# Eight images through a spectral network and a dilation on one core: one more pair of the mixing inside layer 3, and ten head steps behind it in a new order

## The chip, the cores and the metric

The kernel runs on one core of a Trainium2 chip, all in float32. The metric is the device time of one execution in microseconds (us). Five engines work side by side, each through its own list of instructions: TensorE (PE: matrix multiplications; PEld: its weight loads), VectorE (DVE), ScalarE (ACT), GpSimd (POOL) and SyncE (SP). In this kernel SyncE and GpSimd only issue DMAs, but for the setup.

## The reference, cut to what matters

The input has eight images of 8 channels and 256 x 256 pixels. Each goes through a group norm, a network of four spectral layers with a two-stage head, a residual addition, and then another group norm and a 3 x 3 dilation with a second residual addition.

```python
h = _gconv1x1(concat(group_norm(x), grid), fc0_w, fc0_b)      # 40 channels in 4 groups
for i in range(4):
    h1 = irfft2(mix(low modes of rfft2(h), sp_w1[i], sp_w2[i]))   # 12 + 12 rows, 12 columns of modes
    h2 = _gconv1x1(h, w_w[i], w_b[i])
    h = h1 + h2
    if i < 3:
        h = _gswish(h, betas[i])
x = x + _gconv1x1(_gswish(_gconv1x1(h, fc1_w, fc1_b), betas[3]), fc2_w, fc2_b)
x = x + max over 3 x 3 neighbours of group_norm(x), border -2
```

## The kernel before

**Images and layers.** An image's hidden state `h` lies whole in SBUF, in 11 chunks. In each layer `burst(c)` makes a chunk: matrix multiplications with the state (L587 in layer 0, L590 later) and the inverse column transform (L593), then the activation on ScalarE (L598, or L600 in layer 3) back into `h`. In layers 0 to 2 transposes and forward transforms follow (L541, L558, L572). Between two layers stands the spectrum: `spectrum_h` (in front of layer 0, `spectrum_x`), then `mix`, which works out the product of modes and weights, then `rows_even` or `rows_odd`, which make the row transforms (p_g, L487 or L509) and copy them to `zt` (L215 to L217).

**The mixing.** `mix` has twelve operations on VectorE, n = 0 to 11, six pairs of a product (L411) and a sum (L414) of about 1 us each; then six small additions and subtractions that make `fs` (L432, L433); then the multiplications p_f (L455, L464) and copies into `fz` (L465 to L471).

**The head.** Layer 3 stores each chunk of its result to DRAM (L602). The head of that image reads it again as hidden states (L789: 44 of them in all, each for three first steps) and runs while the layers of the next image run. It has 128 *first* steps (`f`) and 64 *second* steps (`c` or `C`). A first step multiplies a state by the first weights into four banks of PSUM (L813) and applies the activation on ScalarE in two pieces, one bank (L814) and three banks (L815). A second step multiplies two activations by the second weights into one bank (L830). An addition on VectorE then takes this bank up into `y` (L837 where a row block begins, L839 else). With `c` the addition is put on VectorE's list at once; with `C` it waits in `sums_due` and is put there at the next first step, or at the next `c`. After each eighth addition statistics (L845) and a write to DRAM (L847, from GpSimd) follow.

**PSUM.** Its eight banks are two single ones (tag `one`) and two triples (tag `tri`), each used in turn. A first step takes one of each, a second step a single, p_f and the first row transform one of each. A user waits until the one two before it has been read.

**Who runs when.** `layers` is a generator for an image. Its yields are strings such as "ffc", and for each letter the main loop calls `step`, which runs a first or a second step of the oldest head that still has some; "t" runs a piece of the dilation of an image whose head is done. The lists of TensorE, VectorE, ScalarE and SyncE are in the order in which this program issues instructions; nothing reorders them later.

**The next image inside layer 3.** `start(b + 1, nxt)` is a second generator: `spectrum_x` and then `mix` with l = 0 of the next image, cut to pieces by its own yields, whose values don't matter here. `rows_odd` of layer 3 runs two of its pieces, and each chunk of layer 3 runs two more (two `next(side, None)` per chunk): 24 in all. What is left then runs in `rest`, behind layer 3: a piece, the head steps of `REST` for that place, some reads of the next image's pixels into the free chunks of `h` (`read_x`, L532, four DMAs a chunk, from SyncE), and so on. Layer 3 itself reads chunks 0 to 6 of the next image when a head runs beside it; for image 0, where none does, all 11 chunks are read in `rest`.

In the kernel before, 20 pieces are `spectrum_x` (the last of them is empty: two yields follow each other at its end, L353 and L354), four pieces hold the pairs n = 0,1 to 6,7, then four pieces hold one operation each (n = 8, 9, 10, 11), one the six additions, and the last one p_f and what follows. So `rest` begins with n = 8. The head steps in it, for images 1 to 6, are `f`, `fc`, `ffC`, `ff`, `fc`. The first `f` and the first `c` are the last of the old head; all others are of the new one.

Of the kernel before, what the change touches and what calls it, by code (L numbers as in the profile page):

```python
# [34 lines left out]
NCH = 11  # L35
# [4 lines left out]
DR = 2  # L40
STEPS = 128
BEHIND = mybir.DependencyInfo(mybir.DependencyClass.Sync, mybir.DependencyReason.DATA)
REST = ("ff", "f", "f", "fC", "fc"), ("f", "fc", "ffC", "ff", "fc")


@with_exitstack
def fno_dilate_kernel(ctx: ExitStack, tc: tile.TileContext, a: dict, out: bass.AP):
# [11 lines left out]
    def ps_a(name):  # L59
        return ps.tile([128, 512], F32, tag="one", bufs=2, name=name)  # L60
# [8 lines left out]
    def part(i):  # L69
        return slice(32 * i, 32 * i + 32)  # L70


    n_img = a["x"].shape[0]
    turned = const.tile([128, 3, 2048], F32, tag="turned", name="turned")

    def load_x(b):
        for i in range(2):
            nc.sync.dma_start(turned[:, i], a["xw"][b, :, i])
# [169 lines left out]
    def rsqrt(v, r, d):  # L248

        nc.vector.tensor_scalar(r.bitcast(I32), v.bitcast(I32), -0.5, float(0x5F3759DF), ALU.mult, ALU.add)  # L250
        nc.vector.tensor_scalar(v, v, -0.5, None, ALU.mult)
        for _ in range(4):
            nc.vector.tensor_tensor(d, r, r, ALU.mult)
            nc.vector.tensor_tensor(d, d, v, ALU.mult)
            nc.vector.scalar_tensor_tensor(r, d, 1.5, r, ALU.add, ALU.mult)


    def group_means(p, v):

        mm(p[:, 0:G], avg, v, start=True, stop=True)  # L260
        for g in range(G):
            mm(p[part(g), G : G + 1], avg[:, 0:32], v[:, g : g + 1], start=True, stop=True)


    def spectrum_x(b, out_):

        x = turned[:, 0:2].rearrange("p i (g f) -> p i g f", g=G)
        st = sb.tile([128, G, 2, 6], F32, tag="bn", bufs=1, name=f"bn_x{b}")
        for i in range(2):
            for g in range(G):  # L270
                nc.vector.bn_stats(st[:, g, i, :], x[:, i, g])
            yield
        mv = sb.tile([128, G, 2], F32, tag="mvx", name=f"mv_x{b}")
        for g in range(G):
            nc.vector.bn_aggr(mv[:, g], st[:, g].rearrange("p n s -> p (n s)"))
        yield
        yield
        yield
        p = ps_a(f"p_st_x{b}")
        group_means(p, mv[:, :, 0])  # L280
        mr = sb.tile([128, 2, G + 1], F32, tag="mrx", name=f"mr_x{b}")
        d = sb.tile([128, 2, G + 1], F32, tag="dx", bufs=1, name=f"d_x{b}")
        nc.vector.tensor_copy(mr[:, 0], p[:, : G + 1])
        dm = d[:, 0, :G]
        nc.vector.tensor_tensor(dm, mv[:, :, 0], mr[:, 0, :G], ALU.subtract)
        nc.vector.tensor_tensor(dm, dm, dm, ALU.mult)
        nc.vector.tensor_tensor(dm, dm, mv[:, :, 1], ALU.add)
        yield
        yield
        q = ps_a(f"p_sv_x{b}")  # L290
        group_means(q, dm)
        nc.vector.tensor_scalar(d[:, 1], q[:, : G + 1], EPS, None, ALU.add)
        rsqrt(d[:, 1], mr[:, 1], d[:, 0])
        out_["mr"] = mr[:, :, G]
        for g in range(G):
            nc.vector.tensor_scalar(
                x[:, :, g], x[:, :, g], mr[:, 0, g : g + 1], mr[:, 1, g : g + 1], ALU.subtract, ALU.mult)
            if g != 1:
                yield
        yield  # L300

        a1, a2 = turned[:, 2, 0:512], turned[:, 2, 512:1024]
        a3 = turned[:, 2, 1024:1216].rearrange("p (g m) -> p g m", g=G)
        nc.vector.memset(a3, 0.0)
        p = ps_a(f"p_a1_{b}")
        for i in range(2):
            for g in range(G):
                mm(p[part(g)], er[:, i, :], x[:, i, g], start=i == 0, stop=i == 1)
        nc.vector.tensor_copy(a1, p)
        yield  # L310
        yield
        t = ps_a(f"p_a2_{b}")
        for i in range(4):
            nc.tensor.transpose(t[:, 128 * i : 128 * (i + 1)], a1[:, 128 * i : 128 * (i + 1)], ident)
        nc.vector.tensor_copy(a2, t)
        yield
        yield
        p = ps_a(f"p_a3_{b}")
        for j in range(2):
            for i in range(2):  # L320
                mm(p[:, 24 * j : 24 * j + 24], a2[:, 256 * j + 128 * i : 256 * j + 128 * i + 128], fw[:, i, 0:24],
                   start=i == 0, stop=i == 1)
        for g in range(G):
            nc.vector.tensor_copy(a3[part(g), g, :], p[part(g), 0:48])
        yield
        yield
        cols = a3.rearrange("p g (j k) -> p g j k", j=2)
        p = ps_a(f"p_xs_{b}")
        for k in range(2):
            for term in range(2):  # L330
                for q in range(4):
                    k0 = 12 * term + 3 * q
                    mm(p[part(q), 24 * k : 24 * k + 24], unf[:, spectrum_table(k, term), :],
                       cols[:, :, :, k0 : k0 + 3], start=term == 0, stop=term == 1)
        xe4 = xe.rearrange("p (s k) g j -> p s g j k", s=2)
        for k in range(2):
            nc.vector.tensor_copy(
                xe4[:, k, :, 0:2, :],
                p[:, 24 * k : 24 * k + 24].rearrange("p (g j k) -> p g j k", g=G, j=2),
            )  # L340
        yield
        bt = sb.tile([128, 2, 3, G, WID], F32, tag="B", bufs=1, name=f"B_{b}_0")
        prod = turned[:, 0, :1200].rearrange("p (i g o j) -> p i g o j", i=6, g=G, o=WID)
        for i in range(6):
            nc.vector.tensor_tensor(
                prod[:, i], wext, xe[:, i].unsqueeze(2).to_broadcast([128, G, WID, 5]), ALU.mult
            )
        nc.vector.tensor_reduce(
            bt.rearrange("p s k g o -> p (s k g o)"),
            prod.rearrange("p i g o j -> p (i g o) j"), AX.X, ALU.add,  # L350
        )
        out_["bt"] = bt
        yield  # L353
        yield  # L354

    def spectrum_table(k, term):

        return 0 if k == term else (1 if k == 0 else 2)
# [44 lines left out]
    def mix(b, l, out_):  # L403
# [3 lines left out]
        for n in range(12):  # L407
            k, k2 = n // 4, n // 2 % 2
            pr = turned[:, 2, 1024 * k2 : 1024 * k2 + 800].rearrange("p (g m i) -> p g m i", g=G, i=WID)
            if n % 2 == 0:  # L410
                nc.vector.tensor_tensor(  # L411
                    pr, sw[k], bt[:, k2, k].unsqueeze(2).to_broadcast([128, G, 2 * WID, WID]), ALU.mult)
            else:
                nc.vector.tensor_reduce(  # L414
                    s[k2][:, k].rearrange("p s o g -> p (s o) g"),
                    pr.rearrange("p g m i -> p m g i"), AX.X, ALU.add,
                )
            if l == 0:
                if n % 2 or n > 7:
                    yield  # L420
            elif n not in (0, 2, 6, 10):
                yield {1: "fc", 4: "fC", 7: "fC", 9: "fC"}.get(n, "f")
            if n == 2 and l == 3 and b + 1 < n_img:
                load_x(b + 1)
# [104 lines left out]
    def read_x(b, c):  # L529
        if b < n_img:  # L530
            for g in range(G):
                nc.sync.dma_start(h[32 * g : 32 * g + 6, c].rearrange("p f w -> p (f w)"), a["xp"][b, c, g])  # L532
# [140 lines left out]
    def start(b, out_):  # L673
        if b < n_img:
            if b == 0:
                out_["sw"] = [load_sw(0, k) for k in range(3)]
            yield from spectrum_x(b, out_)
            yield from mix(b, 0, out_)

    def rest(b, then):  # L680
        c = 0 if b == 0 else NCH - 4
        for n, _ in enumerate(then):
            yield REST[b > 0][n]
            for _ in range(2 if b == 0 else 1):
                if c < NCH:
                    read_x(b + 1, c)
                    c += 1
        for i in range(c, NCH):
            read_x(b + 1, i)

    def layers(b, stored, d, then, ahead):

        for l in range(4):
            if l > 0:
                yield from spectrum_h(b, l, d)
                yield from mix(b, l, d)
            yield from rows_odd(b, l, then) if l % 2 else rows_even(b, l)  # L700
            yield from layer(b, l, d, stored, then, ahead)
        yield "stored"
        yield from rest(b, then)
# [420 lines left out]
```

## Time and profile before

| what | us |
|---|---|
| median of 3 runs (lowest, highest) | 3690.49 (3689.13, 3691.84) |
| the profiled execution: its time, its span | 3688.73, 3687.0 |
| PE busy | 3486.2 |
| ACT busy | 2865.0 |
| DVE busy | 2386.8 |
| one product of the mixing (L411), one sum (L414), mean | 0.983, 0.984 |
| one addition of the head (L839), mean | 0.684 |
| activation of a first step: L814, L815, mean | 0.602, 1.458 |

Times in the profile count from the start of the span. A line of the timeline gives the start, the length from the first to the last of the merged instructions, the engine and the line of the kernel, the operation, what it writes and reads, how many were merged, and in brackets how long the engine was idle before and what ended this. SPq is SyncE's queue; the length of its issues holds what it waits between them. An engine that waits for several things has the wait put down to the one that came last.

### The profile page before, as it was taken

The numbers are of one execution on the slowest core, as the hardware profiler recorded it, in microseconds if no ns is written. First come the engines' busy times: TensorE is split into PE (matmuls) and PEld (weight loads), VectorE is DVE, ScalarE is ACT, GpSimd is POOL, SyncE is SP. The second block draws the span as 40 slices with busy tenths as digits, with TensorE's granted clock in tenths as the row PEclk, the third lists the DMA queues.
The fourth block names the chain that finished last, engine by engine and source line by source line (L and its number), as shares of the span: only waits on it lengthen the run. The fifth ranks groups of instructions, "written<-read, shape, count | busy, mean of one in ns | idle before, by whom it ended". The sixth has DMA issues, their size and how long they took to land.

```text
span 3687.0 us, 112658 instructions
## 1 busy us (share of the span) xinstructions
PE 3486.2 (95%) x50872; PEld 1270.1 (34%) x50872; DVE 2386.8 (65%) x3711; ACT 2865.0 (78%) x3021; POOL 117.1 (3%) x202
## 2 busy tenths in 40 slices
PE   5768999999999999999999999999999999999997
PEld 2323333333333333333333333333333333333222
DVE  6776666557775677757776577765777567772443
ACT  2436888888788788787888888888888888889986
POOL 1000000000000000000000000000000000000000
PEclk7879999999999999999999999999999999999998
DMA  3005111532226212271224512253222521225221
GB/s 92 16 17 212 49 50 46 165 106 72 72 84 195 68 58 72 87 226 53 65 57 138 170 55 75 64 168 114 67 73 89 189 75 58 71 65 193 84 82 48
DMA packets 114080, 344.71 MB, mean 93 GB/s; under 512 B 15984, under 2 KB 18480, under 8 KB 98176
## 3 DMA queue, kind: packets, MB, share of 16 engines
q1 hardware_dynamic: 95392, 276.32, 24.5%
q0 software_dynamic: 18208, 61.18, 5.1%
q8 instruction: 400, 6.55, 0.7%
q14 instruction: 80, 0.66, 0.1%
HBM read 213.44 MB, written 123.74 MB: 91 GB/s over the span
## 4 chain that ended last, share of the span: by engine, by line
PE 73%; DVE 16%; issue 5%; ACT 4%; DMA 2%; POOL 0%; ACTq 0%; DVEq 0%; POOLq 0%
PE p_fc L830 20%; PE p_fc L813 19%; PE p_z L593 9%; PE p_d L558 7%; PE p_z L590 7%; PE p_z L587 3%; DVE y L839 3%; PE p_u L572 3%; DVE turned L541 3%; DVE S L414 3%; DVE turned L411 2%; DMA yin<-y_rows 2%; DVE turned L372 1%; PE p_b L381 1%; PE p_g L509 1%
## 5 line engine op out<-in xcount | busy, mean ns | idle before, releaser
L815 ACT ACTIVATE act<-p_fc 128x1536 f32<-128x1536 f32 x1024 | 1493.2, 1458 | 0.0
L813 PE MATMUL p_fc<-hs,c_w 32*128 32x512 f32 x8192 | 1133.4, 625 | 41.2 <-DVE y L839 20.8
L830 PE MATMUL p_fc<-act,c_w 128*32 128x512 f32 x8192 | 1007.0, 600 | 0.2 <-ACT act L815 0.2
L814 ACT ACTIVATE act<-p_fc 128x512 f32<-128x512 f32 x1024 | 616.6, 602 | 228.2 <-PE p_fc L813 216.8
L541 DVE STREAM_TRANSPOSE turned<-h 128x1024 f32<-128x1024 f32 x528 | 632.6, 1226 | 189.7 <-ACT h L598 189.0
L598 ACT ACTIVATE h<-p_z 128x512 f32<-128x512 f32 (+1 forms) x528 | 511.9, 1021 | 213.9 <-PE p_z L593 213.9
L839 DVE TENSOR_TENSOR y<-p_fc,y 128x512 f32<-128x512 f32 x392 | 267.9, 684 | 539.1 <-PE p_fc L830 539.1
L813 PEld LDWEIGHTS p_fc<-hs,c_w 32*128 32x128 f32 x8192 | 358.3, 183 | 613.4 <-ACT act L814 253.3
L830 PEld LDWEIGHTS p_fc<-act,c_w 128*32 128x32 f32 x8192 | 221.4, 109 | 703.9 <-issue 330.8
L593 PE MATMUL p_z<-c_binv,zt 32*128 32x256 f32 x5632 | 410.3, 405 | 0.0
L590 PE MATMUL p_z<-h,c_wt 32*32 32x512 f32 x8448 | 357.8, 601 | 7.9 <-ACT act L814 4.2
L593 PEld LDWEIGHTS p_z<-c_binv,zt 32*128 32x128 f32 x5632 | 258.9, 186 | 308.0 <-issue 295.1
L558 PE MATMUL p_d<-turned,c_fw 32*32 32x480 f32 (+1 forms) x9216 | 307.6, 539 | 0.6 <-DVE turned L541 0.2
L562 ACT ACTIVATE turned<-p_d 128x1440 f32<-128x1440 f32 x144 | 183.0, 1271 | 89.5 <-PE p_d L558 86.3
L600 ACT ACTIVATE h<-p_z,c_bias 128x512 f32<-128x512 f32 (+1 forms) x176 | 186.4, 1110 | 72.0 <-PE p_z L593 71.8
L215 ACT ACTIVATE zt<-p_g 128x198 f32<-128x198 f32 (+2 forms) x118 | 53.4, 575 | 182.7 <-PE p_g L487 99.9
L414 DVE TENSOR_REDUCE S<-turned 128x80 f32<-128x800 f32 x192 | 189.0, 984 | 5.9
L411 DVE TENSOR_TENSOR turned<-t,B 128x800 f32<-128x800 f32 x192 | 188.7, 983 | 0.9
L558 PEld LDWEIGHTS p_d<-turned,c_fw 32*32 32x32 f32 x9216 | 127.1, 103 | 165.6 <-issue 64.7
L372 DVE STREAM_TRANSPOSE turned<-zt 128x960 f32<-128x960 f32 x96 | 176.8, 1867 | 2.5
L590 PEld LDWEIGHTS p_z<-h,c_wt 32*32 32x32 f32 x8448 | 92.9, 103 | 175.3 <-DVE y L839 48.8
L572 PE MATMUL p_u<-turned,c_stack 128*32 128x480 f32 (+1 forms) x1152 | 136.7, 543 | 11.5 <-DVE turned L561 6.2
(192 smaller groups left out, 1763.1 us busy)
## 6 DMA issues: line engine op xcount, KB each, us to landing
stored<-h SPq DMA_DIRECT2D x88, 1024.0 KB
hs<-stored SPq DMA_DIRECT2D x352, 256.0 KB
t<-in_spw SPq DMA_DIRECT2D x96, 400.0 KB
yin<-y_rows POOLq DMA_DIRECT2D x56, 512.0 KB, 5.2
h<-in_xp SPq DMA_DIRECT2D x352, 48.0 KB
turned<-in_xw SPq DMA_DIRECT2D x16, 1024.0 KB
y<-in_x SPq DMA_DIRECT2D x56, 256.0 KB
y_rows<-y POOLq DMA_DIRECT2D x56, 256.0 KB, 4.0
```

What stands on the lines that cost most here:

```text
L411: nc.vector.tensor_tensor(pr, sw[k], bt[:, k2, k].unsqueeze(2).to_broadcast([128, G, 2 * WID, WID]), ALU.mult)
L414: nc.vector.tensor_reduce(s[k2][:, k].rearrange("p s o g -> p (s o) g"), pr.rearrange("p g m i -> p m g i"), AX.X, ALU.add,)
L541: nc.vector.transpose(dst[:, 2 * i : 2 * i + 2], h[:, c, 2 * i : 2 * i + 2].rearrange("p f (s x) -> p f s x", s=2))
L558: mm(banks[q][part(v % 4), : 240 * n], fw8[part(q), v, :], t[part(q), :, :, v, : NBLK * WID], start=v < 4, stop=v >= 4)
L590: mm(o, wt[part(q), l, g, :], h[part(q), c, f, :], start=True, stop=False)
L593: mm(banks[q][:, HW * s : HW * (s + 1)], zt[part(q), 2 * c + s].rearrange("p f o -> p (f o)"), binv[part(q), :], start=False, stop=s == 1)
L598: nc.scalar.activation(dst, src, AF.Silu)
L813: mm(banks[g], w1[part(g), blk, :], hs[k][part(g), :], start=True, stop=True)
L814: nc.scalar.activation(act[:, 0, :], one, AF.Silu)
L815: nc.scalar.activation(act[:, 1:4, :], tri, AF.Silu)
L830: mm(acc[part(g), :], w2[:, g, 15 - rb - i : 47 - rb - i], act[:, g, :], start=i == 0, stop=i == 1)
L839: nc.vector.tensor_tensor(y, sums, y, ALU.add)
```

## The change

Three edits. `spectrum_x` loses its second closing yield, so the empty piece is gone. In `mix` with l = 0 a yield comes only after each sum, so that n = 8, 9 are one piece and n = 10, 11 another; with both, the 24 pieces inside layer 3 reach to n = 9 instead of n = 7. Behind layer 3 three pieces are left (n = 10, 11; the six additions; p_f and what follows). `rest` is written for these: head steps first, then four chunks of reads, then the piece. For images 1 to 6 the order of the ten head steps, with the pieces in brackets, goes from

```
[8] f [9] f c [10] f f C [11] f f [additions] f c [p_f]
```

to

```
f f c [10 11] f f [additions] C f f c f [p_f]
```

For image 7, which has no next image, `rest` returns at once; it had no pieces before either.

```diff
-REST = ("ff", "f", "f", "fC", "fc"), ("f", "fc", "ffC", "ff", "fc")
+REST = ("fff", "ff", "Cfc"), ("ffc", "ff", "Cffcf")
...
         out_["bt"] = bt
         yield
-        yield
...
             if l == 0:
-                if n % 2 or n > 7:
+                if n % 2:
                     yield
...
         c = 0 if b == 0 else NCH - 4
-        for n, _ in enumerate(then):
+        if b + 1 == n_img:
+            return
+        for n in range(3):
             yield REST[b > 0][n]
-            for _ in range(2 if b == 0 else 1):
-                if c < NCH:
-                    read_x(b + 1, c)
-                    c += 1
-        for i in range(c, NCH):
-            read_x(b + 1, i)
+            for i in range(c + 4 * n, min(c + 4 * n + 4, NCH)):
+                read_x(b + 1, i)
+            next(then, None)
```

The edits shorten the file: behind `spectrum_x` a line of the changed kernel has a number smaller by one, behind `rest` by two (first step L811, its activations L812 and L813, second step L828, additions L835 and L837).

## The prediction

> **What bounds the kernel now.** I read the page first, then the table of stretches around the passage from one image to the next (image 0 last), then the waits inside one such stretch, then the timeline of VectorE and TensorE in it.
>
> ```profile
> PE 3486.2 (95%) x50872; PEld 1270.1 (34%) x50872; DVE 2386.8 (65%) x3711; ACT 2865.0 (78%) x3021; POOL 117.1 (3%) x202
> L813 PE MATMUL p_fc<-hs,c_w 32*128 32x512 f32 x8192 | 1133.4, 625 | 41.2 <-DVE y L839 20.8
> ...
> 755.13:787.96 32.83, 30.44 (x337) 10.45 (x333) 21.71 (x40) 25.58 (x29) 1.31 (x2) 1.00 0.57 167
> 1192.17:1226.65 34.48, 32.09 (x336) 10.88 (x332) 21.70 (x40) 25.58 (x29) 1.30 (x2) 0.95 0.59 159
> 1633.35:1666.17 32.82, 30.43 (x336) 10.44 (x332) 21.68 (x40) 25.57 (x29) 1.30 (x2) 1.00 0.57 167
> 327.16:354.55 27.39, 26.06 (x289) 9.67 (x285) 18.97 (x35) 21.86 (x25) 0.00 (x0) 1.00 0.64 224
> ...
> PE p_fc L813 <- DVE y L839: 2.0, 2, 1.8
> ```
>
> TensorE is busy 95% of the span, so only what keeps it waiting can be won. The columns of the stretches are length, then busy PE, PEld, DVE, ACT, POOL, clock, DMA share, GB/s. Each goes from the last burst of layer 3 to the first burst of the next image. Those of images 1 to 6 are alike to 0.01 us (4 to 6, not shown, are 32.82, 32.83 and 32.82), but for image 2, where 3.41 us at half clock fall (0.95). In each of the six (in the waits of image 1: 1.8 the longest) a first step of the head waits 1.81 us for an addition on VectorE. Why is seen here:
>
> ```profile
> 750.32 1.40 DVE L348 TENSOR_REDUCE B<-turned 128x240 f32<-128x1200 f32 x1
> 754.17 0.69 DVE L839 TENSOR_TENSOR y<-p_fc,y 128x512 f32<-128x512 f32 x1 [2.45 <-PE p_fc L830]
> ...
> 763.95 0.99 DVE L414 TENSOR_REDUCE S<-turned 128x80 f32<-128x800 f32 x1
> 764.85 0.98 DVE L411 TENSOR_TENSOR turned<-t,B 128x800 f32<-128x800 f32 x1
> 765.87 0.99 DVE L414 TENSOR_REDUCE S<-turned 128x80 f32<-128x800 f32 x1
> 766.77 0.68 DVE L839 TENSOR_TENSOR y<-p_fc,y 128x512 f32<-128x512 f32 x1
> ...
> 762.71 1.92 PE L830 MATMUL p_fc<-act,c_w 128*32 128x512 f32 x16
> 764.56 1.14 PE L813 MATMUL p_fc<-hs,c_w 32*128 32x512 f32 x8
> 767.51 1.14 PE L813 MATMUL p_fc<-hs,c_w 32*128 32x512 f32 x8 [1.81 <-DVE y L839]
> 768.58 1.92 PE L830 MATMUL p_fc<-act,c_w 128*32 128x512 f32 x16
> ```
>
> The second step (L830) ends near 764.6, but its addition L839 stands behind three pairs of the mixing (L411, L414) and starts at 766.77. It frees one of the two single banks of PSUM, and the second first step after it needs that bank: 767.51. Earlier, from 751.72 to 754.17, VectorE is idle for 2.45 us.
>
> **What the Trainium skill says.** Perfetto Trace Analysis, section Tensor Engine Instruction: ScalarE, VectorE and GpSimd queues are strict FIFOs, and TensorE's ends are modelled. The trace agrees: the addition doesn't pass the pairs. The same page, Identifying Performance Opportunities: a gap that repeats can mean too little PSUM for the next tile; the same 1.81 us stand in all six passages. TensorE: Matmul & The Clock Gate, Part 1: half clock follows an idle window of some 3.4 us. The trace has half-clock intervals of 3.41 us; whether idle time brings them, it can't tell (the same stall in the five other passages has none).
>
> **The change, step by step** (times of image 1; I call the ten head steps f1 f2 c1 f3 f4 C2 f5 f6 f7 c3 before; after it is f1 f2 c1 f3 f4 C2 f5 f6 c3 f7, by the order of each engine's instructions).
>
> Image 0: the order on all engines is the same as before, its eight steps and SyncE's issues included (five first steps come first either way, and no addition falls due among the pairs). 0 us. Image 7 has no image behind it: 0.
>
> The empty piece: at chunk 8 of layer 3 the second slot was empty and now holds the first pair. It takes 1.95 us (0.98 + 0.99, less overlap) from 751.72, to about 753.7; the addition of chunk 9 is ready only at 754.17. Hidden by the idle 2.45 us with 0.4 us to spare. Chunks 9 and 10 hold two pairs each as before. If the pair had to wait more than 0.4 us for its table, the rest would be paid per image; the tables were issued at 700 to 713 us, so I take 0 (bounds 0 and 1.5 us: the pair less the spare).
>
> The last pair but one leaves the ten steps. VectorE is then free at 764.85 instead of 766.77. c1's addition is ready 2.00 us after c1 starts (c3 at 774.64, addition at 776.64), 764.70. So it starts at 764.85, 1.92 earlier, and f4 at 765.63: right behind f3 at the usual 1.07 us (767.51 to 768.58). The stall is gone: 1.88 us.
>
> What is late next: ScalarE takes 1.81 us for a first step (773.41 to 775.22) and starts it 1.16 us after TensorE does (764.56 to 765.72). A first step needs the triple bank of the one two before. Going on from 765.63: C2 766.70; f5 768.55 (1.85 after a second step); VectorE does the statistics 765.57, the last pair 766.18 to 768.18, then the six subtractions and additions (0.88 us) to 769.1, and only then C2's addition, put behind them by the new order: 769.05 to 769.78. f6 needs its bank: 769.84, a wait of 0.2 us where 1.07 spacing would be 769.62. ScalarE meanwhile: f3 765.72, f4 767.53, f5 769.71, f6 771.53.
>
> The swap: c3 goes ahead of f7. c3 at 770.91; it needs f5's activation in its second half at 771.9, done at 771.65: no wait (up to 0.3 if the semaphore is slow). f7 at 772.8; its banks are free (772.13 and 771.65). p_f at 773.87 against 776.50: 2.63 earlier. But ScalarE starts f7 only at 773.96 and ends it at 775.9, where before it ended at 777.20, that is 0.70 after p_f's start, and now 2.0 after. The next first step f8 needs f7's triple bank; it would start at 775.08 and goes on at 775.95. So 0.87 us of the 2.63 are paid back: 1.76 there (777.71 against 775.95). Following it: f9 777.0, the second step 777.9 (779.63), the row transform p_g 779.8 (781.49), each 1.6 to 1.8 earlier; the zt copies on VectorE and the first burst follow these. I take 1.7 us per passage, with 1.5 and 2.6 as bounds (2.6: the payback hidden).
>
> SyncE: before, four reads of the next image (four issues each) with loads of hidden states between them: read 7, state 3, read 8, 9, state 4, read 10; after, state 3, reads 7 to 10, state 4. State 3 goes earlier. State 4 went at 772.30, and now goes behind read 10, whose last issue ended at 775.08: some 3 us later. It is used by the thirteenth first step at 803.91, 28 us later, and state 3 had to do with 20 us (766.49 to 786.49). Hidden: 0. The reads are used a chunk at a time in layer 0, from 788 us on. GpSimd's write of the finished rows stands behind c1's addition and starts 1.9 us earlier: 0 or a little gain.
>
> Sum: six passages by 1.7 us = 10.2 us. Against the profiled execution (3688.73 us, its span 3687.0) that is a span of 3676.8 and 3678.5 in all; that execution lies 1.8 under the median of the runs, 3690.49, so the forecast is 3680.3.
>
> **Rivals.** (1) The payback is hidden, the passage keeps all 2.63: 6 x 2.63 = 15.8, 3674.7. For it speaks that ScalarE is idle 1.73 us before f8 now; against it that f8 can't start before f7's banks are read. (2) The stall isn't the addition's: another releaser keeps f4 at 767.5. Then the swap alone remains; p_f stays, and f8 waits some 0.87 us for f7: 6 x 0.87 = 5.2 slower at worst, 3690.5 to 3695.7, no difference that counts. Against it: the start follows the addition's by 0.74 us in all six, as f6 follows its own addition (770.57, 771.38) by 0.81. A gain of half the size would fall here too. (3) Slower: SyncE's queue. State 4, behind sixteen reads in a row that wait for the stores of layer 3, comes after its turn. It decides from 27 us after its issue; each us beyond costs one per image. At 5 us beyond, less 1.7 gained, 6 x 3.3 = 20 slower: 3710. Against it the 28 us of room, and that SyncE's four reads took 2.1 to 2.6 us each. (4) Clock: one more half-clock interval costs 1.7 us (half of 3.41), one less gains as much; image 2's stretch is 1.65 longer than the others and its interval starts just behind the stall. This widens the range by some 3 us only.
>
> **How the numbers follow.** Forecast 0.70, rival 1 0.09, rival 2 0.14, rival 3 and the like (the moved pair exposed) 0.07. What this kernel's measurement tells from no change is 0.2%, 7.4 us: under 3683.1 is faster, above 3697.9 slower. Faster: 0.70 + 0.09, less 0.02 for a forecast cut by clock intervals, 0.77; same 0.14 + 0.02 + 0.01 of rival 3, 0.17; slower 0.06. The range goes from rival 1 (3674) to a gain of 4.5 us (3686): it leaves out rival 3 and most of rival 2.
>
> **What would show it.** In the changed kernel's stretches: 31.1 us instead of 32.8 in images 1 to 6, image 0 still 27.4; no wait of 1.8 us at f4 on L839 (there two lines earlier, L837); c1's addition right behind the fourth pair; p_f 2.6 earlier against the last burst; f8's rest about 0.9 behind f7's activation; the first pair at chunk 8 ahead of the addition without delaying it. I am wrong if the stretches keep 32.8, if the wait comes back at f6 or f8 in full, or if time is lost outside these stretches, at the thirteenth first step above all.

## The result, and the profile after

The changed kernel takes 3678.11 us (median of 7 runs, 3676.95 to 3682.24) against 3690.49 us (median of 7, 3689.13 to 3696.24): the ratio is 0.9965, with a 95% interval of 0.9954 to 0.9977. It is faster by 12.4 us (by the interval 8.5 to 17.0), where 10.2 were forecast. The profiled execution has a span of 3675.3 us, 11.7 under that of before. In the changed kernel first steps are L811 (activations L812, L813), second steps L828, their additions L835 and L837, pairs of the mixing L410 and L413, and p_f L454.

The table of stretches of the changed kernel, from the first multiplication of layer 3's last burst to the first one of the next image, for images 1, 2, 6 and 0. The columns are length, then busy PE, PEld, DVE, ACT, POOL, clock, DMA share, GB/s:

```profile
755.05:786.15 31.10, 30.51 (x336) 10.41 (x332) 19.90 (x38) 25.68 (x29) 1.31 (x2) 1.00 0.61 177
1191.09:1222.19 31.10, 30.51 (x337) 10.40 (x333) 19.90 (x38) 25.68 (x29) 1.30 (x2) 1.00 0.64 177
...
2937.21:2968.30 31.09, 30.50 (x336) 10.41 (x332) 19.93 (x38) 25.67 (x29) 1.30 (x2) 1.00 0.65 176
326.93:354.31 27.38, 26.05 (x288) 9.66 (x284) 18.96 (x35) 21.84 (x25) 0.00 (x0) 1.00 0.63 223
```

Each of the six passages is 31.1 us long where it was 32.8, and image 0's is unchanged. TensorE's busy time in them stays (30.5 against 30.4): what went is waiting. Image 2's stretch has gained 1.65 us more, since no half-clock interval falls in it now (in this profile one of 6.83 us begins 3.3 us behind image 5's stretch). The six together have lost 12.0 us (198.6 to 186.6), which is the whole change of the span but for 0.4 us.

VectorE in the changed kernel, from chunk 8 of layer 3 on (the timeline: start, length, instruction, and in brackets the idle time before it and what ended it):

```profile
750.24 1.40 DVE L348 TENSOR_REDUCE B<-turned 128x240 f32<-128x1200 f32 x1
751.67 0.99 DVE L410 TENSOR_TENSOR turned<-t,B 128x800 f32<-128x800 f32 x1
752.70 0.99 DVE L413 TENSOR_REDUCE S<-turned 128x80 f32<-128x800 f32 x1
754.09 0.69 DVE L837 TENSOR_TENSOR y<-p_fc,y 128x512 f32<-128x512 f32 x1 [0.40 <-PE p_fc L828]
...
763.87 0.98 DVE L413 TENSOR_REDUCE S<-turned 128x80 f32<-128x800 f32 x1
764.77 0.68 DVE L837 TENSOR_TENSOR y<-p_fc,y 128x512 f32<-128x512 f32 x1
```

The first pair sits in the old idle time and leaves 0.40 us of it, so the addition of chunk 9 isn't late. c1's addition follows the fourth pair at 764.77. TensorE then runs:

```profile
764.48 2.17 PE L811 MATMUL p_fc<-hs,c_w 32*128 32x512 f32 x16
766.58 2.11 PE L828 MATMUL p_fc<-act,c_w 128*32 128x512 f32 x16
768.62 2.25 PE L811 MATMUL p_fc<-hs,c_w 32*128 32x512 f32 x16
770.79 2.03 PE L828 MATMUL p_fc<-act,c_w 128*32 128x512 f32 x16
772.76 1.14 PE L811 MATMUL p_fc<-hs,c_w 32*128 32x512 f32 x8
773.83 0.88 PE L454 MATMUL p_f<-fs,c_fold 32*32 32x72 f32 x64
774.64 0.25 PE L463 MATMUL p_f<-c_wbd,dc 128*32 128x12 f32 x8
774.82 3.08 PE L811 MATMUL p_fc<-hs,c_w 32*128 32x512 f32 x16
777.83 1.92 PE L828 MATMUL p_fc<-act,c_w 128*32 128x512 f32 x16
```

f3 and f4 stand together without a gap. The x16 group of first steps right behind p_f (f8 and f9) takes 3.08 us. In the kernel before it took 2.00:

```profile
776.50 0.88 PE L455 MATMUL p_f<-fs,c_fold 32*32 32x72 f32 x64
777.52 0.25 PE L464 MATMUL p_f<-c_wbd,dc 128*32 128x12 f32 x8
777.71 2.00 PE L813 MATMUL p_fc<-hs,c_w 32*128 32x512 f32 x16
779.64 1.92 PE L830 MATMUL p_fc<-act,c_w 128*32 128x512 f32 x16
```

This is the payback of the swap, f8 waiting for the banks of f7.

### The profile page after: what moved, and what is told of

It is laid out like the page before. It is cut to its first block, busy times and chain, and to the rows that moved or that the text cites. A ratio compares the mean times of both kernels' runs of the same rounds, so it can differ in the third digit from the quotient of the medians.

```text
span 3675.3 us, 112628 instructions
## 1 busy us (share of the span) xinstructions
PE 3483.8 (95%) x50872; PEld 1269.2 (35%) x50872; DVE 2387.8 (65%) x3711; ACT 2865.8 (78%) x3021; POOL 117.0 (3%) x202
## 4 chain that ended last, share of the span: by engine, by line
PE 74%; DVE 15%; issue 5%; ACT 4%; DMA 2%; POOL 0%; ACTq 0%; DVEq 0%; POOLq 0%
PE p_fc L828 20%; PE p_fc L811 20%; PE p_z L592 9%; PE p_d L557 7%; PE p_z L589 7%; PE p_z L586 3%; DVE turned L540 3%; PE p_u L571 3%; DVE y L837 3%; DVE S L413 2%; DVE turned L410 2%; DMA yin<-y_rows 2%; DVE turned L371 1%; PE p_g L508 1%; PE p_b L380 1%
## 5 line engine op out<-in xcount | busy, mean ns | idle before, releaser
L813 ACT ACTIVATE act<-p_fc 128x1536 f32<-128x1536 f32 x1024 | 1492.9, 1458 | 3.1 <-PE p_fc L811 3.1
L811 PE MATMUL p_fc<-hs,c_w 32*128 32x512 f32 x8192 | 1131.7, 625 | 29.1 <-DVE y L837 10.0
L828 PE MATMUL p_fc<-act,c_w 128*32 128x512 f32 x8192 | 1008.1, 600 | 0.2 <-ACT act L813 0.2
L812 ACT ACTIVATE act<-p_fc 128x512 f32<-128x512 f32 x1024 | 616.3, 602 | 214.1 <-PE p_fc L811 201.6
L837 DVE TENSOR_TENSOR y<-p_fc,y 128x512 f32<-128x512 f32 x392 | 267.8, 683 | 525.0 <-PE p_fc L828 525.0
L811 PEld LDWEIGHTS p_fc<-hs,c_w 32*128 32x128 f32 x8192 | 355.9, 183 | 601.7 <-ACT act L812 259.2
L828 PEld LDWEIGHTS p_fc<-act,c_w 128*32 128x32 f32 x8192 | 222.6, 109 | 703.9 <-issue 331.0
L413 DVE TENSOR_REDUCE S<-turned 128x80 f32<-128x800 f32 x192 | 189.0, 984 | 5.9
L410 DVE TENSOR_TENSOR turned<-t,B 128x800 f32<-128x800 f32 x192 | 188.7, 983 | 1.1
```

The costliest lines, as they stand in the source:

```text
L410: nc.vector.tensor_tensor(pr, sw[k], bt[:, k2, k].unsqueeze(2).to_broadcast([128, G, 2 * WID, WID]), ALU.mult)
L413: nc.vector.tensor_reduce(s[k2][:, k].rearrange("p s o g -> p (s o) g"), pr.rearrange("p g m i -> p m g i"), AX.X, ALU.add,)
L811: mm(banks[g], w1[part(g), blk, :], hs[k][part(g), :], start=True, stop=True)
L812: nc.scalar.activation(act[:, 0, :], one, AF.Silu)
L813: nc.scalar.activation(act[:, 1:4, :], tri, AF.Silu)
L828: mm(acc[part(g), :], w2[:, g, 15 - rb - i : 47 - rb - i], act[:, g, :], start=i == 0, stop=i == 1)
```

## The experiments

In the expectations the stretch is counted from the start of the last multiplication of L593 in the last burst to the next image's first burst. Counted so, it is 30.70 us before and 28.98 us in the changed kernel; the tables begin 2.12 us earlier. Theory 1 is the prediction's: the time comes from c1's addition no longer standing behind a third pair on VectorE's list. Its rivals: the new order of the head steps brings it (theory 2), or the pair has to leave the stretch because VectorE has too much work there (theory 3).

### The pair kept out of layer 3

```diff
@@ spectrum_x
         yield
+        yield
@@ rest
+        next(then, None)
         for n in range(3):
```

> The changed kernel, but layer 3 ends with the pair n = 6,7 again and n = 8,9 run behind it, ahead of the ten steps in the new order. Against the changed kernel only VectorE's order differs. Theory 1 (the time comes from the addition of c1 no longer standing behind a third pair): the 1.8 us wait of f4 is back, p_f some 0.1 us from where it was before, the stretch of images 1 to 6 is 30.6 to 31.0 us, the time within 2 us of the kernel before's apart from clock intervals. Theory 2 (the new order of the head steps, f7 behind c3, brings it): stretch near 29.0 us, the time about 12 us under the kernel before.

The ratio to the kernel before is 0.9999 (0.9990 to 1.0008): nothing is left of the gain. Here are the timeline of TensorE and the waits in image 1's stretch of this run:

```profile
763.99 1.92 PE L830 MATMUL p_fc<-act,c_w 128*32 128x512 f32 x16
765.84 1.14 PE L813 MATMUL p_fc<-hs,c_w 32*128 32x512 f32 x8
768.79 1.14 PE L813 MATMUL p_fc<-hs,c_w 32*128 32x512 f32 x8 [1.81 <-DVE y L839]
...
PE p_fc L813 <- DVE y L839: 2.0, 2, 1.8
```

The wait is back at f4 with its 1.81 us. The stretch is 30.78 us in the four passages without a half-clock interval: 0.08 longer than before. The new order and the new place of the reads win nothing while the addition stands behind the third pair. Theory 2 falls.

### Two pairs ahead of the steps

```diff
@@ rest (and the second closing yield of spectrum_x, as above)
+        next(then, None)
+        next(then, None)
         for n in range(3):
             yield REST[b > 0][n]
             ...
-            next(then, None)
+            if n:
+                next(then, None)
```

> As the run before, but n = 8,9 and n = 10,11 both stand ahead of the ten steps, so that c1's addition has one more pair in front of it: the suspected wait is doubled. Theory 1: f4 waits 1.8 + 1.95 = 3.7 us, the stretch is 30.7 + 1.95 = 32.7 us (32.2 to 32.9), six of them 10 to 12 us over the kernel before. Theory 2: no difference from the changed kernel, 29.0 us.

The ratio is 1.0059 (1.0044 to 1.0074): 3712.74 us, 21 us over the kernel before where 10 to 12 were expected. The wait has the expected size, in the timeline of TensorE:

```profile
765.70 1.14 PE L815 MATMUL p_fc<-hs,c_w 32*128 32x512 f32 x8
770.57 2.09 PE L815 MATMUL p_fc<-hs,c_w 32*128 32x512 f32 x8 [3.73 <-DVE y L841]
```

and the stretches show what came on top; the clock is the third number from the end:

```profile
756.28:792.64 36.36, 32.05 (x336) 10.62 (x332) 21.78 (x40) 25.78 (x29) 1.31 (x2) 0.95 0.51 152
1197.59:1235.11 37.52, 33.21 (x337) 10.82 (x333) 21.79 (x40) 25.79 (x29) 1.30 (x2) 0.91 0.49 146
```

f4 itself takes 2.09 us instead of 1.14. The trace's clock record has a half-clock interval of 3.41 us that begins as the wait ends (770.6), and there is one in each of the six passages (6.83 us long in two). A passage with 3.41 us of it is 3.54 us longer than an undisturbed one before: 1.92 by the wait, and the other 1.6 goes with the clock. The six together are 22.1 us longer than in the profile of before (220.7 against 198.6), which is the 21 us. So theory 1 had the wait right and missed the half clock that comes with such a wait.

### The pairs between the steps

```diff
-REST = ("fff", "ff", "Cfc"), ("ffc", "ff", "Cffcf")
+REST = ("", "fff", "ff", "Cfc"), ("ffc", "ffc", "ff", "cf")
@@ rest (and the second closing yield of spectrum_x, as above)
-        for n in range(3):
+        for n in range(4):
             yield REST[b > 0][n]
-            for i in range(c + 4 * n, min(c + 4 * n + 4, NCH)):
+            k = n - (b == 0)
+            for i in range(c + 4 * k, min(c + 4 * k + 4, NCH)) if k >= 0 else ():
                 read_x(b + 1, i)
```

> No pair more inside layer 3 than in the kernel before (empty piece kept); behind it f f c [8 9] f f c [10 11] f f [additions] c f [p_f], each head addition at once. Theory 1: c1's addition finds VectorE free at the end of n = 7 as in the changed kernel, the f4 wait is gone, and C2's addition is earlier too; stretch 28.8 us (28.6 to 29.1), the time that of the changed kernel. Theory 3 (the pair must leave the ten steps, since VectorE's work in the stretch is what counts): stretch 30 us or more, the time of the kernel before.

The ratio is 0.9970 (0.9959 to 0.9980), 3678.32 us: the changed kernel's time. Its stretch in image 1, and VectorE's timeline there:

```profile
757.84:788.94 31.10, 30.52 (x336) 10.43 (x332) 21.87 (x40) 25.68 (x29) 1.31 (x2) 1.00 0.61 177
...
766.66 0.99 DVE L414 TENSOR_REDUCE S<-turned 128x80 f32<-128x800 f32 x1
767.56 0.68 DVE L839 TENSOR_TENSOR y<-p_fc,y 128x512 f32<-128x512 f32 x1
768.28 0.69 DVE L845 BATCH_NORM_STATS2 bn_y<-y 128x6 f32<-128x512 f32 x1
768.89 0.97 DVE L411 TENSOR_TENSOR turned<-t,B 128x800 f32<-128x800 f32 x1
```

VectorE is busy 21.87 us in the stretch, as it was before (21.71; the changed kernel has 19.90), and yet the stretch is as short as the changed kernel's. Theory 3 falls: what counts is that the addition stands ahead of the pair, not where the pair is done. Counted from L593 it is 28.98 us, not the 28.8 that I expected from C2's earlier addition. TensorE's timeline shows where that went:

```profile
771.41 2.07 PE L813 MATMUL p_fc<-hs,c_w 32*128 32x512 f32 x16
773.41 2.21 PE L830 MATMUL p_fc<-act,c_w 128*32 128x512 f32 x16
```

f5 and f6 are done 0.18 us sooner than in the changed kernel (2.07 us against 2.25), but c3 takes 0.18 longer (2.21 against 2.03). Its second half starts 14.60 us after L593 in both kernels, 0.05 us behind the end of f5's activation on ScalarE, so it waits for that either way. p_f then comes as in the changed kernel, 16.66 us after L593.

### The swap undone

```diff
-REST = ("fff", "ff", "Cfc"), ("ffc", "ff", "Cffcf")
+REST = ("fff", "ff", "Cfc"), ("ffc", "ff", "Cfffc")
```

> The changed kernel with f7 ahead of c3 again; against the changed kernel only TensorE's order differs. Theory 1: f7's three banks wait for f5's activation some 0.8 us, p_f comes about 0.75 us later than in the changed kernel, but f8 waits for nothing, so the stretch is 28.85 us (28.7 to 29.1 against 28.98): the swap is worth nothing. Theory 2: the stretch goes back to 30 us or more.

The ratio is 0.9967 (0.9957 to 0.9976), and the stretch 28.97 us. TensorE's timeline in image 1:

```profile
769.25 4.28 PE L811 MATMUL p_fc<-hs,c_w 32*128 32x512 f32 x24
773.46 1.92 PE L828 MATMUL p_fc<-act,c_w 128*32 128x512 f32 x16
775.32 0.88 PE L454 MATMUL p_f<-fs,c_fold 32*32 32x72 f32 x64
776.34 0.25 PE L463 MATMUL p_f<-c_wbd,dc 128*32 128x12 f32 x8
776.52 2.00 PE L811 MATMUL p_fc<-hs,c_w 32*128 32x512 f32 x16
```

Three first steps in a row take 4.28 us, 1.07 more than three of 1.07; f8 and f9 then take 2.00 again. In the changed kernel f8 and f9 take 1.08 more. The wait is the same in size and only stands elsewhere, so the swap is worth nothing.

### Half a pair more, and the clock

```diff
@@ mix
-                if n % 2:
+                if n % 2 or n == 10:
@@ rest (and the second closing yield of spectrum_x, as above)
+        next(then, None)
+        next(then, None)
         for n in range(3):
```

> Behind layer 3 the three operations n = 8, 9, 10 stand ahead of the ten steps in the new order, n = 11 behind c1. A step between the two runs that kept one pair and two pairs out. Theory 1: f4 waits 1.8 + 1.0 = 2.8 us in images 1 to 6. Theory 4 on the clock (each wait of 3.7 us of TensorE was followed by 3.4 us at half clock, and one or two in six of those of 1.8 us): with 2.8 us more of the six passages than two, but not all, have a half-clock interval just behind the wait, and the undisturbed stretch (from the last burst's second half, L593, to the first burst) is 31.8 us. If the clock intervals fall anywhere, no more passages have one than at 1.8 us.

A single run took 3698.85 us, beside a median of 3691.59 of the kernel before. Two stretches and f4 in the first of them:

```profile
756.44:791.82 35.38, 32.09 (x337) 10.50 (x333) 21.80 (x40) 25.80 (x29) 1.31 (x2) 0.95 0.54 155
1196.00:1229.73 33.73, 30.44 (x337) 10.32 (x333) 21.78 (x40) 25.79 (x29) 1.30 (x2) 1.00 0.57 162
...
769.72 1.19 PE L814 MATMUL p_fc<-hs,c_w 32*128 32x512 f32 x8 [2.71 <-DVE y L840]
```

The wait is 2.71 us in all six passages, and five of them have a half-clock interval right behind it (clock 0.95); the second here has none and is 1.65 us shorter. Within the stretches of all these profiles, of 12 passages with a wait of 1.81 us three have such an interval, of six with 2.71 us five, of six with 3.73 us all, and of the 24 without the wait (the changed kernel twice, the pairs between, the swap undone) none.

But the stretches end at the next image's first burst, and the clock record goes on. Behind 9 of those 24 passages an interval begins 3.3 to 3.9 us after that burst, and so it does behind 2 of the 12 with 1.81 us. With these counted, 9 of 24 passages without the wait have half clock, and 4 of 12 with the wait of 1.81 us. So a wait of 2.71 or 3.73 us came with an interval in 11 of 12 passages. For 1.81 us the profiles show none more than without a wait, only that one can fall inside the stretch and not behind it. They show the coincidence and its price, not the rule of the throttle.

### A try to lift the floor

p_f goes ahead of f7, and f8, c4, f9 follow:

```diff
-REST = ("fff", "ff", "Cfc"), ("ffc", "ff", "Cffcf")
+REST = ("fff", "ff", "Cfc"), ("ffc", "ff", "Cffc")
@@ rows_even
-        yield "ffc"
+        early = l == 0 and b > 1
+        yield "ffcf" if early else "ffc"
...
-            yield "fcf"[oi]
+            yield ("cff" if early else "fcf")[oi]
```

> The changed kernel, with f7 moved behind p_f in images 2 to 7, then f8 c4 f9 ahead of the first row transform, and behind the transforms c, f, f in place of f, c, f (the counts are the same). Theory 1 with the floor found so far (a first step cannot start its three banks sooner than 3.1 us after the first step two users of the triples before): f8 no longer waits for f7's activation, the first row transform comes 0.5 to 0.7 us earlier, the stretch of the passages into images 2 to 7 is 28.2 to 28.9 us against 28.98, the time 1 to 4 us under the changed kernel's. Rival: the same wait comes back at f9 or at the step behind the transform, and the stretch is 29.0 us or more.

3683.61 us, ratio 0.9978 (0.9970 to 0.9987); the changed kernel on the same chip has 0.9970 (below). The stretch is longer, not shorter, 29.84 us from L593. This is TensorE's timeline in image 1:

```profile
775.05 2.00 PE L812 MATMUL p_fc<-hs,c_w 32*128 32x512 f32 x16
...
780.21 0.64 PE L487 MATMUL p_g<-c_rowg,fz 32*128 32x264 f32 x8
781.06 2.41 PE L829 MATMUL p_fc<-act,c_w 128*32 128x512 f32 x16 [0.20 <-ACT act L813]
...
785.82 0.72 PE L487 MATMUL p_g<-c_rowg,fz 32*128 32x264 f32 x6 [0.84 <-DVE zt L217]
```

The wait behind p_f is gone (2.00), and the first row transform comes 21.94 us after L593 instead of 22.51, as theory 1 said. But the last transform waits 0.84 us for the copies to `zt`, and the second step ahead takes 2.41 us: the rival is right, and the time is lost again behind the transform. No version here beats the changed kernel.

### The changed kernel again

Nothing is edited.

> The changed kernel once more, on the same chip as these runs. Theory 1: stretches 28.98 us in images 1 to 6, 12 us under the kernel before, of which 10.3 us in the passages and the rest from half-clock intervals that it has less of.

3678.70 us, ratio 0.9970 (0.9958 to 0.9981), stretches of 28.96 to 28.98 us and no half-clock interval in the passages, but one behind each of the last two.

## Why the prediction was right

**The stall's cause.** Right, and shown by dose: with the third pair ahead of c1's addition f4 waits 1.81 us, with half a pair more 2.71, with a whole one 3.73, and with the addition first (in two ways) nothing. The repeating gap did not come from too few banks of PSUM: with the same banks it went when the addition came first.

**The hand-made schedule.** It gave p_f 2.63 us earlier; it came 2.59 earlier (16.66 against 19.25 us after L593). It gave a payback of 0.87 at f8: of the 2.59 us, 1.73 are left at the second step behind f9 (20.66 against 22.39 us after L593), so 0.86 were paid back. The group of f8 and f9 lasted 1.08 longer, but began 2.81 earlier. It gave 1.7 us a passage, and the passages gained 1.72. The 0.4 us to spare at chunk 8 are 0.40. Two parts of the change were not needed for it: with the swap undone, or with the pair left behind layer 3 after the addition, the stretch is as short (28.97 and 28.98 us from L593).

**What was costed at nothing.** Image 0's stretch is 27.38 us, as before. SyncE's new order cost nothing: in the changed kernel state 4 goes at 774.41 and the thirteenth first step runs at 802.12 with no wait, and with the pair kept out the whole new order costs 0.08 us a passage. Rivals 1, 2 and 3 are all out.

**What the sum leaves open.** The six passages without the clock give 10.3 us, as forecast. The measured change is 12.4 us, and its interval of 8.5 to 17.0 holds both. The medians of the three later runs without the stall (the pairs between, the swap undone, the changed kernel again) lie 13.1, 10.8 and 12.9 us under that of before. So some 2 us outside the sum are likely, and no experiment here shows where they come from.

The clock, taken in the prediction as an even chance of some 3 us either way, is the candidate. The granted clock was recorded for 54 runs with the 1.81 us wait and for 30 without it: the means are 0.9782 and 0.9786. An estimate from these, over the whole span, is 3.4 us less of half clock without the stall, which is 1.7 us of time with a standard error of 0.8. The profiles don't confirm it: passages with the 1.81 us wait have no more half clock, in them and just behind, than those without. So that part is not shown.

**The clock page.** The prediction cites the Trainium skill's page TensorE: Matmul & The Clock Gate (Part 1) for half clock after an idle window of some 3.4 us. The intervals here do last 3.41 us or a multiple of it, but waits of 1.8 and 2.7 us were followed by them too. Those behind the passages began with no wait ahead of them: in the pairs between, TensorE was busy for 6.82 of the 6.82 us up to 792.78, and half clock began at 792.79. Where page and trace differ, the measurement decides.

## What to carry to other kernels

Where an in-order engine takes up PSUM for the bound engine and also does slack work, look at the order on its list before its load (here the stretch lost its wait with VectorE's work in it unchanged): put the take-up ahead of the slack work that is in no hurry. Read such a stall in the timeline of the engine that is blamed, between the moment when its input was ready and the start of the instruction that frees the buffer. Before a swap of steps is priced by the first instruction that comes earlier, follow it to the next user of the same buffers: 2.6 us became 1.7.

## What was unexpected of the hardware

A long wait of TensorE cost more than its length. Six waits of 3.73 us, where 1.81 were before, added 11.5 us by themselves and 21 us in all; the rest goes with the half clock that came with each, 3.41 us or more. At 2.71 us five of six came with it. And half clock came without a wait as well: behind 9 of the 24 passages where the stall was gone it began 3.3 to 3.9 us into the next image's first layer.
